# A recurrent scan step on Trainium2: one square moved to ScalarE, four activations reordered, and a common factor taken once

## The chip, the cores and the metric

The kernel runs on one core of a Trainium2 chip, as one program in one launch. The metric is the device time of a whole execution in microseconds (us). The engines are named as in the profile: PE is TensorE's matmul and PEld its weight load, DVE is VectorE, ACT is ScalarE, POOL is GpSimd and SP is SyncE. Each engine works through its own queue of instructions in order, and engines wait for each other (and for their own earlier results) on semaphores.

## What is computed

The reference is a small network of eight sublayers over x of 2 x 2048 x 256 numbers, in float32. The change touches only the first one, a gated scan over time. Its step, cut to what matters (h holds a complex number, as two real parts, for each of 2 batches, 256 channels d and 16 states n; there are 2048 steps):

```python
def step(h, inp):
    x_t, dt_t, B_t, C_t, xr_t = inp
    h_carrier = h.mean(axis=1)
    T = jnp.cos((c_phase(xr_t) - c_phase(h_carrier)) / 2.0) ** 2
    alpha = jnp.exp(dt_t[..., None] * A_neg)
    expo = 1.0 + (1.0 - alpha) * KAPPA * (1.0 - T[:, None, :])
    mag, ph = (c_mag(h), c_phase(h))
    cmag = jnp.minimum(jnp.exp(expo * jnp.log(mag + 1e-08)), 10.0)
    h = from_polar(cmag, ph)
    Bx = B_t[:, None, :, :] * (dt_t * x_t)[:, :, None, None]
    h = h + Bx
    h = from_polar(jnp.tanh(c_mag(h)), c_phase(h))
    y_t = jnp.einsum('bnc,bdnc->bd', C_t, h)
    return (h, y_t)
```

The lines of interest are the last three: a new h, here called p in the kernel, keeps its direction and gets the length tanh(|p|). The kernel computes this without angles. With m = |p| and e = exp(-2m), tanh(m) = (1 - e) / (1 + e), so the new h is p times (1/|p|) times (1 - e) times 1/(1 + e).

## The kernel before

The program goes through its sublayers one after the other: the tables for the scan, the scan, a projection, then routers, attention-like sublayers, a long convolution and feed-forward layers. Only the scan (`scan`, L257 to L549) and in it `step` (L400 to L488) is of interest here.

**Layout.** The 128 partitions hold batch, state and a quarter of the channels; the 64 columns (J) hold the channels of that quarter. Every tile of a step is 128 x 64, or 128 x 2 x 64 for the two parts of a complex number, and most instructions of a step work on 128 x 64 numbers.

**Order.** Steps depend on each other, so there are 2048 of them in sequence: a hardware loop (L513) of four passes, each with 32 groups (L517) of 16 unrolled steps (L539). The order of instructions on each engine is the order of the code, since the loop's body is under `manual_schedule`. Loads of the next group's tables are issued by SP at the start of a group. Two hooks fill gaps of a step with work for later steps: `act_gap` (called at L440) lets ACT compute the next step's input term bx (L391, twice) and in half of the steps a quarter of the next group's decay table (L385 or L387, 128 x 256); `dve_gap` (called at L454) lets DVE do small copies in a few steps.

**One step.** It begins with PE summing hs, the sums over channels of the last h (L410), and ACT and PE making from it the carrier's scale ci. Meanwhile DVE makes gl, ex and ngd (L414 to L425) from the logarithm lg and correction kd of the last step. ACT exponentiates (ea, fac). DVE forms p (L436 to L444), one instruction for each of the two parts. Then comes the stretch that the change touches:

- DVE: z and q[1], q[0] (squares of the parts, L446 to L449), m2 from z and q[1] (the squared magnitude with its small constant, L451), r1 from q[0] and q[1] (the same without it, L453).
- ACT: lm = ln m2 (L459), lr = ln r1 (L460), m = exp(lm / 2) (L461), ir = exp(-lr / 2), which is 1/|p| (L463), e = exp(-2m) (L464), lb (L466), le = ln(1 + e) (L468; its tile bears the name of m), sg = exp(-le), which is 1/(1 + e) (L469), then rm, k2c, ld and k1 (L470 to L473), which only the next step's lg and kd need.
- DVE: p times ir (L475, both parts), times (e - 1) (L477, both parts), and times sg (L480, both parts), the last with a sum over the columns into hs for the next step. Then th, kc, dl, lg and kd (L484 to L488), which make the logarithm and the correction for the next step.

The tiles lm, m, lr and lb lie in PSUM, the others in SBUF. The timeline of the profile calls the tile of both m and m2 "m", and those of r1 and k1 "r" and "k".

Of the kernel before, what the change touches and what calls it, by code (L numbers as in the profile page):

```python
# [17 lines left out]
AF = mybir.ActivationFunctionType  # L18
ALU = mybir.AluOpType
# [19 lines left out]
MAG_EPS = 1e-8  # L39
# [20 lines left out]
def new(pool, shape, name, **kw):  # L60
    return pool.tile(list(shape), F32, name=name, tag=name, **kw)


class Kernel:
# [192 lines left out]
    def scan(self, y, dtd, dxd, tabd):  # L257
# [7 lines left out]
        V, A, G = nc.vector, nc.scalar, nc.gpsimd  # L265
        J, TURN = 64, TG * GROUPS
        with ExitStack() as c:
# [129 lines left out]
            w = lambda sh, name: new(wp, [P, *sh], name)  # L397
            wa = lambda name: new(pa, [P, J], name)

            def step(k, g, before, act_gap, dve_gap):  # L400

                tc_, ng, dx, cs = tg[g]
                ng = ng[:, k]
                h = hist[g][:, k - 1] if k else hist[1 - g][:, TG - 1]
                hn = hist[g][:, k]
                i, o = (k + 1) % 2, k % 2

                for out in (hc, hd):
                    for r in range(0, P, 32):
                        nc.tensor.matmul(out[r : r + 32], mean[:, r : r + 32], hs[i], start=True, stop=True)  # L410
                before()

                gl, ex, ea, ngd = (w([J], n) for n in ("gl", "ex", "ea", "ngd"))
                V.tensor_tensor(gl, lg[i], ng, ALU.mult)  # L414


                sq, n2c = w([2], "sq"), w([1], "n2c")
                A.activation(sq, hc, AF.Square, accum_out=n2c)  # L418
                junk, dot = w([2], "junk"), w([1], "dot")
                V.tensor_tensor_reduce(  # L420
                    out=junk, in0=hd, in1=tc_[:, 4:6, k], scale=1.0, scalar=0.0, op0=ALU.mult, op1=ALU.add,
                    accum_out=dot,
                )
                V.tensor_tensor(ex, kd[i], gl, ALU.subtract)  # L424
                V.tensor_scalar(ngd, gl, dot, None, ALU.mult)  # L425
                ln, ci = wa("lr")[:, 0:1], w([1], "ci")
                A.activation(ln, n2c, AF.Ln, bias=1e-18)
                A.activation(ci, ln, AF.Exp, scale=-0.5)
                A.activation(ea, ex, AF.Exp)  # L429


                nc.tensor.matmul(hd[32:33, 0:1], ci, self.ident[:, 0:1], start=True, stop=True)  # L432


                p = w([2, J], "p")
                V.scalar_tensor_tensor(p[:, 0], h[:, 0], SMALL, ea, ALU.add, ALU.mult)  # L436
                V.tensor_tensor(p[:, 1], h[:, 1], ea, ALU.mult)  # L437
                fac = w([J], "fac")
                A.activation(fac, ngd, AF.Exp, scale=ci)  # L439
                act_gap(k)  # L440
                for k2 in range(2):
                    V.tensor_tensor(p[:, k2], p[:, k2], fac, ALU.mult)  # L442
                for k2 in range(2):
                    V.tensor_tensor(p[:, k2], p[:, k2], bx[o][:, k2], ALU.add)  # L444
                z = w([J], "z")
                V.scalar_tensor_tensor(z, p[:, 0], -2.0 * SMALL, p[:, 0], ALU.add, ALU.mult)  # L446
                q = w([2, J], "q")
                V.tensor_tensor(q[:, 1], p[:, 1], p[:, 1], ALU.mult)
                V.tensor_tensor(q[:, 0], p[:, 0], p[:, 0], ALU.mult)  # L449
                m2 = w([J], "m2")  # L450
                V.scalar_tensor_tensor(m2, z, MAG_EPS, q[:, 1], ALU.add, ALU.add)  # L451
                r1 = w([J], "r1")
                V.scalar_tensor_tensor(r1, q[:, 0], 1e-19, q[:, 1], ALU.max, ALU.add)  # L453
                dve_gap(k)  # L454

                lm, m, lr = wa("lm"), wa("m"), wa("lr")
                A.activation(lm, m2, AF.Ln)  # L459
                A.activation(lr, r1, AF.Ln)  # L460
                A.activation(m, lm, AF.Exp, scale=0.5)  # L461
                ir, e, sg, rm, ld = (w([J], n) for n in ("ir", "e", "sg", "rm", "ld"))
                A.activation(ir, lr, AF.Exp, scale=-0.5)  # L463
                A.activation(e, m, AF.Exp, scale=-2.0)  # L464
                lb, k1, k2c = wa("lb"), w([J], "k1"), w([J], "k2c")
                A.activation(lb, m2, AF.Ln, bias=MAG_EPS)  # L466
                le = wa("m")
                A.activation(le, e, AF.Ln, bias=1.0)  # L468
                A.activation(sg, le, AF.Exp, scale=-1.0)  # L469
                A.activation(rm, lm, AF.Exp, scale=-1.0)  # L470
                A.activation(k2c, lb, AF.Exp, scale=-0.5)
                A.activation(ld, e, AF.Ln, scale=-1.0, bias=1.0)  # L472
                A.activation(k1, rm, AF.Ln, scale=MAG_EPS, bias=1.0)  # L473
                for k2 in range(2):
                    V.tensor_tensor(p[:, k2], p[:, k2], ir, ALU.mult)  # L475
                for k2 in range(2):
                    V.scalar_tensor_tensor(p[:, k2], e, -1.0, p[:, k2], ALU.add, ALU.mult)  # L477
                th, kc, dl = (w([J], n) for n in ("th", "kc", "dl"))
                for k2 in range(2):
                    V.tensor_tensor_reduce(  # L480
                        out=hn[:, k2], in0=p[:, k2], in1=sg, scale=-1.0, scalar=0.0 if k2 else J * SMALL,
                        op0=ALU.mult, op1=ALU.add, accum_out=hs[o][:, k2 : k2 + 1],
                    )
                V.tensor_tensor(th, ld, le, ALU.subtract)  # L484
                V.scalar_tensor_tensor(kc, k2c, 2.0 * MAG_EPS, k1, ALU.mult, ALU.add)
                V.scalar_tensor_tensor(dl, hn[:, 0], -SMALL, rm, ALU.mult, ALU.mult)
                V.scalar_tensor_tensor(lg[o], th, 2.0, kc, ALU.mult, ALU.add)
                V.scalar_tensor_tensor(kd[o], kc, 0.5, dl, ALU.mult, ALU.add)  # L488
# [24 lines left out]
            with tc.For_i(0, S, TURN) as iv:  # L513
                A.preload_act_table_set(LOG_EXP)
                with tc.manual_schedule():
                    late = None
                    for g in range(GROUPS):  # L517
# [4 lines left out]
                        def act_gap(k):  # L522
                            for k2 in range(2):
                                if k + 1 < TG:
                                    drive(j, k + 1, k2, (k + 1) % 2)
                                else:
                                    drive(nxt, 0, k2, 0)
                            if k == 1:
                                rows(iv + (g + 1) * TG, nxt)
                            if 3 <= k < 11:  # L530
                                decay(nxt, (k - 3) // 2 * 4, 4, (k - 3) % 2)

                        def dve_gap(k):
                            if k == 1 and late is not None:
                                outputs(*late)
                            if k in (3, 4):
                                picked(nxt, k - 3)

                        for k in range(TG):  # L539
                            def before():  # L540
                                if k:
                                    project(j, k - 1, yps)
                                elif late is not None:
                                    project(1 - j, TG - 1, late[1])

                            step(k, j, before, act_gap, dve_gap)
# [1223 lines left out]
```

## Time and profile before

| what | value |
|---|---|
| time, median of 3 runs | 13,714.66 us (13,710.65 to 13,725.5) |
| the profiled execution's own time | 13,713.61 us |
| span of its trace | 13,711.9 us |
| DVE busy | 10,653.5 us, 78% of the span |
| ACT busy | 9,294.0 us, 68% |
| PE busy | 5,477.8 us, 40% |
| first and last start of L480 (the scan) | 370.5 and 10,034.5 us |

The shares are averages over the whole program. A row of a group gives the line, the engine, the operation, the tiles written and read, the shapes and the count; behind the first bar the busy time in all and the mean of one in ns; behind the second the idle time of the engine just before, and what ended it. A row of the timeline gives the start in us, the duration in us, engine, line, operation and tiles; in brackets the idle time before it. The span of an instruction on DVE or ACT overlaps that of the next one, so the distance from start to start, not the duration, is what an instruction occupies of its engine.

### The profile page before, as it was taken

What the parts mean: (1) busy time and instruction counts of PE and PEld (TensorE: products, weight loads), DVE (VectorE), ACT (ScalarE), POOL (GpSimd) and SP (SyncE); (2) the same over time, 40 slices, a digit from 0 to 9 for tenths busy, and PEclk for the clock granted to TensorE, in tenths of its full rate; (3) what the DMA queues carried; (4) which work ended last, traced back from release to release, by engine and by line L of the source; (5) the groups of instructions that cost most, each with busy time, mean ns of one, the idle gap of its engine ahead of it and who ended that gap; (6) DMA issues with size and microseconds to landing.
All of it is one profiled execution on the core that took longest, in us unless ns stands there. A gap on an engine that the chain in (4) does not pass through costs nothing. (4 is left out here: it accounts for less than half of the span.)

```text
span 13711.9 us, 263042 instructions
## 1 busy us (share of the span) xinstructions
PE 5477.8 (40%) x66344; PEld 3762.0 (27%) x66344; DVE 10653.5 (78%) x65491; ACT 9294.0 (68%) x45234; POOL 460.9 (3%) x528
## 2 busy tenths in 40 slices
PE   4222222222222222222222222222269867778888
PEld 2111111111111111111111111111135545644445
DVE  6888888888888888888888888888857677655555
ACT  3777777777777777777777777777735478534444
POOL 0000000000000000000000000000000001131110
PEclk6555555555555555555555555555559888889999
DMA  3000000000000000000000000000000045242210
GB/s 81 14 14 17 14 17 15 17 16 15 17 14 17 14 17 14 17 14 17 14 17 17 14 16 15 17 14 17 14 13 4 7 134 155 73 94 34 35 31 19
DMA packets 320440, 382.28 MB, mean 28 GB/s; under 512 B 207074, under 2 KB 230697, under 8 KB 317876
## 3 DMA queue, kind: packets, MB, share of 16 engines
q1 hardware_dynamic: 299444, 322.01, 10.2%
q0 software_dynamic: 17408, 42.75, 1.0%
q8 instruction: 533, 8.73, 0.3%
q14 instruction: 1007, 8.25, 0.2%
q10 hardware_dynamic: 2048, 0.53, 0.0%
HBM read 307.96 MB, written 52.46 MB: 26 GB/s over the span
## 5 line engine op out<-in xcount | busy, mean ns | idle before, releaser
L410 PE MATMUL hc<-hs,mean 128*32 128x2 f32 x16384 | 586.1, 203 | 7096.9 <-DVE hs L480 7033.2
L410 PEld LDWEIGHTS hc<-hs,mean 128*32 128x32 f32 x16384 | 410.6, 140 | 7308.9 <-DVE hs L480 7244.7
L475 DVE TENSOR_TENSOR p<-p,ir 128x64 f32<-128x64 f32 x4096 | 737.4, 221 | 1062.9 <-ACT ir L463 1062.9
L459 ACT ACTIVATE lm<-m 128x64 f32<-128x64 f32 x2048 | 466.2, 228 | 1210.2 <-DVE m L451 1210.2
L493 PE MATMUL yps<-cs,hist 128*64 128x8 f32 x8192 | 1224.9, 259 | 13.0 <-DVE hs L480 13.0
L391 ACT ACTIVATE bx<-dx,tc 128x64 f32<-128x64 f32 x4098 | 1169.4, 332 | 0.1
L1594 ACT ACTIVATE d_p<-ps_e 128x512 f32<-128x512 f32 (+3 forms) x1280 | 599.5, 537 | 754.2 <-PE ps_o L1575 534.8
L493 PEld LDWEIGHTS yps<-cs,hist 128*64 128x64 f32 x8192 | 1033.1, 218 | 45.1 <-DVE hs L480 13.4
L418 ACT ACTIVATE sq<-hc 128x2 f32<-128x2 f32 x2048 | 352.9, 172 | 795.2 <-PE hc L410 795.2
L480 DVE CUSTOM_DVE_ANT_0 hist<-p,sg 128x64 f32<-128x64 f32 x4096 | 761.0, 222 | 23.0 <-ACT rm L470 4.2
L477 DVE SCALAR_TENSOR_TENSOR p<-e,p 128x64 f32<-128x64 f32 x4096 | 738.1, 221 | 9.9 <-ACT sg L469 7.8
L442 DVE TENSOR_TENSOR p<-p,fac 128x64 f32<-128x64 f32 x4096 | 737.4, 221 | 8.9 <-DVE p L437 6.6
L444 DVE TENSOR_TENSOR p<-p,bx 128x64 f32<-128x64 f32 x4096 | 722.2, 218 | 2.6
L439 ACT ACTIVATE fac<-ngd,ci 128x64 f32<-128x64 f32 x2048 | 711.8, 348 | 1.0 <-DVE p L436 1.0
L436 DVE SCALAR_TENSOR_TENSOR p<-hist,ea 128x64 f32<-128x64 f32 x2048 | 459.7, 224 | 323.3 <-ACT ea L429 323.3
L429 ACT ACTIVATE ea<-ex 128x64 f32<-128x64 f32 x2048 | 524.3, 256 | 99.6 <-DVE ex L424 7.0
L1587 PE MATMUL ps_e<-d_qt,d_kt 128*128 128x512 f32 (+3 forms) x1280 | 556.4, 444 | 43.0 <-ACT d_p L1594 34.6
L472 ACT ACTIVATE ld<-e 128x64 f32<-128x64 f32 x2048 | 548.0, 268 | 0.0
L473 ACT ACTIVATE k<-rm 128x64 f32<-128x64 f32 x2048 | 545.0, 266 | 0.0
L410 PE MATMUL hd<-hs,mean 128*32 128x2 f32 x16384 | 543.7, 193 | 0.0
L1544 PE MATMUL ps_m<-d_kt,d_qt 128*128 128x512 f32 (+3 forms) x1280 | 499.3, 436 | 101.3 <-DVE d_part L1549 40.3
L432 PE MATMUL hd<-ident,ci 128*1 128x1 f32 x4096 | 386.7, 163 | 357.2 <-DVE ex L424 303.4
(453 smaller groups left out, 22720.5 us busy)
## 6 DMA issues: line engine op xcount, KB each, us to landing
toep<-in_C_krev SPq DMA_DIRECT2D x256, 312.0 KB, 5.5
ng<-dtd SPq DMA_DIRECT2D x258, 256.0 KB, 3.4
dx<-dxd SPq DMA_DIRECT2D x258, 256.0 KB, 3.9
d_kt<-d_kd SPq DMA_DIRECT2D x128, 128.0 KB, 4.1
d_qt<-d_qd SPq DMA_DIRECT2D x128, 128.0 KB, 3.7
y<-ys SPq DMA_DIRECT2D x512, 8.0 KB, 1.9
c_xd<-c_xs POOLq DMA_DIRECT2D x32, 256.0 KB, 2.6
c_yd<-c_ys POOLq DMA_DIRECT2D x32, 256.0 KB, 4.3
```

Source lines behind the costliest of these rows:

```text
L391: A.activation(bx[o][:, k2], tg[j][2][:, k], AF.Identity, scale=tg[j][0][:, k2, k : k + 1], bias=0.0 if k2 else SMALL,)
L410: nc.tensor.matmul(out[r : r + 32], mean[:, r : r + 32], hs[i], start=True, stop=True)
L439: A.activation(fac, ngd, AF.Exp, scale=ci)
L442: V.tensor_tensor(p[:, k2], p[:, k2], fac, ALU.mult)
L444: V.tensor_tensor(p[:, k2], p[:, k2], bx[o][:, k2], ALU.add)
L472: A.activation(ld, e, AF.Ln, scale=-1.0, bias=1.0)
L475: V.tensor_tensor(p[:, k2], p[:, k2], ir, ALU.mult)
L477: V.scalar_tensor_tensor(p[:, k2], e, -1.0, p[:, k2], ALU.add, ALU.mult)
L480: V.tensor_tensor_reduce(out=hn[:, k2], in0=p[:, k2], in1=sg, scale=-1.0, scalar=0.0 if k2 else J * SMALL, op0=ALU.mult, op1=ALU.add, accu ...
L493: nc.tensor.matmul(yps[:, k, :], hist[g][:, k, k2], tg[g][3][:, k2, k], start=k2 == 0, stop=k2 == 1)
L1587: nc.tensor.matmul(s[:, q0:], ks[kt // 4][:, hh, kt % 4 * P : (kt % 4 + 1) * P], q[:, hh, q0:], start=True, stop=not diag,)
L1594: A.activation(pr[:, q0:], s[:, q0:], AF.Exp, scale=0.25)
```

## The change

The square of the real part is computed by ACT, behind `act_gap`'s work, instead of DVE. On ACT, m comes ahead of lr, e ahead of ir, and le ahead of lb. The two multiplications by ir and the two by (e - 1) become one instruction that makes ai = (e - 1) times ir, and two multiplications by ai. A step so has two instructions fewer on DVE and one more on ACT. Nothing else of the program is changed, and the order on PE, POOL and SP stays as it was.

```diff
                 q = w([2, J], "q")
                 V.tensor_tensor(q[:, 1], p[:, 1], p[:, 1], ALU.mult)
-                V.tensor_tensor(q[:, 0], p[:, 0], p[:, 0], ALU.mult)
+                A.activation(q[:, 0], p[:, 0], AF.Square)
                 m2 = w([J], "m2")
...
                 A.activation(lm, m2, AF.Ln)
+                A.activation(m, lm, AF.Exp, scale=0.5)
                 A.activation(lr, r1, AF.Ln)
-                A.activation(m, lm, AF.Exp, scale=0.5)
                 ir, e, sg, rm, ld = (w([J], n) for n in ("ir", "e", "sg", "rm", "ld"))
+                A.activation(e, m, AF.Exp, scale=-2.0)
                 A.activation(ir, lr, AF.Exp, scale=-0.5)
-                A.activation(e, m, AF.Exp, scale=-2.0)
                 lb, k1, k2c = wa("lb"), w([J], "k1"), w([J], "k2c")
-                A.activation(lb, m2, AF.Ln, bias=MAG_EPS)
                 le = wa("m")
                 A.activation(le, e, AF.Ln, bias=1.0)
+                A.activation(lb, m2, AF.Ln, bias=MAG_EPS)
                 A.activation(sg, le, AF.Exp, scale=-1.0)
...
+                ai = w([J], "ai")
+                V.scalar_tensor_tensor(ai, e, -1.0, ir, ALU.add, ALU.mult)
                 for k2 in range(2):
-                    V.tensor_tensor(p[:, k2], p[:, k2], ir, ALU.mult)
-                for k2 in range(2):
-                    V.scalar_tensor_tensor(p[:, k2], e, -1.0, p[:, k2], ALU.add, ALU.mult)
+                    V.tensor_tensor(p[:, k2], p[:, k2], ai, ALU.mult)
                 th, kc, dl = (w([J], n) for n in ("th", "kc", "dl"))
```

## The prediction

> **What bounds the kernel now.** I read the page first: the span, and the costliest groups with what ended the idle time before them. Slices 2 to 30 of the page look alike, and the lines with x2048 and x4096 are the scan, so one step, 2048 times over, decides. The table of waits then shows a closed loop (PE waits for DVE's L480, ACT's L459 for DVE, DVE's L475 for ACT): a chain that hops between engines, where no engine is full. So I read one step in the timeline.
>
> ```profile
> span 13711.9 us, 263042 instructions
> ...
> L475 DVE TENSOR_TENSOR p<-p,ir 128x64 f32<-128x64 f32 x4096 | 737.4, 221 | 1062.9 <-ACT ir L463 1062.9
> ```
>
> ```profile
> 5004.20 0.22 DVE L414 TENSOR_TENSOR gl<-lg,ng 128x64 f32<-128x64 f32 x1
> ...
> 5004.45 0.23 DVE L424 TENSOR_TENSOR ex<-kd,gl 128x64 f32<-128x64 f32 x1
> ...
> 5005.67 0.49 ACT L385 ACTIVATE ng<-ng,aneg 128x256 f32<-128x256 f32 x1
> ...
> 5006.01 0.21 DVE L448 TENSOR_TENSOR q<-p 128x64 f32<-128x64 f32 x1
> 5006.15 0.21 DVE L449 TENSOR_TENSOR q<-p 128x64 f32<-128x64 f32 x1
> 5006.28 0.21 DVE L451 SCALAR_TENSOR_TENSOR m<-z,q 128x64 f32<-128x64 f32 x1
> 5006.42 0.21 DVE L453 SCALAR_TENSOR_TENSOR r<-q 128x64 f32<-128x64 f32 x1
> 5006.53 0.23 ACT L459 ACTIVATE lm<-m 128x64 f32<-128x64 f32 x1 [0.37 <-DVE m L451]
> 5006.69 0.21 ACT L460 ACTIVATE lr<-r 128x64 f32<-128x64 f32 x1
> 5006.84 0.18 ACT L461 ACTIVATE m<-lm 128x64 f32<-128x64 f32 x1
> 5006.94 0.21 ACT L463 ACTIVATE ir<-lr 128x64 f32<-128x64 f32 x1
> 5007.06 0.22 ACT L464 ACTIVATE e<-m 128x64 f32<-128x64 f32 x1
> 5007.17 0.23 ACT L466 ACTIVATE lb<-m 128x64 f32<-128x64 f32 x1
> 5007.19 0.36 DVE L475 TENSOR_TENSOR p<-p,ir 128x64 f32<-128x64 f32 x2 [0.56 <-ACT ir L463]
> 5007.31 0.22 ACT L468 ACTIVATE m<-e 128x64 f32<-128x64 f32 x1
> 5007.52 0.36 DVE L477 SCALAR_TENSOR_TENSOR p<-e,p 128x64 f32<-128x64 f32 x2
> 5007.57 0.22 ACT L469 ACTIVATE sg<-m 128x64 f32<-128x64 f32 x1
> 5007.69 0.22 ACT L470 ACTIVATE rm<-lm 128x64 f32<-128x64 f32 x1
> ...
> 5007.89 0.22 DVE L480 CUSTOM_DVE_ANT_0 hist<-p,sg 128x64 f32<-128x64 f32 x1
> ...
> 5008.04 0.27 ACT L473 ACTIVATE k<-rm 128x64 f32<-128x64 f32 x1
> ...
> 5008.34 0.22 DVE L485 SCALAR_TENSOR_TENSOR kc<-k2c,k 128x64 f32<-128x64 f32 x1
> ...
> 5008.89 0.22 DVE L414 TENSOR_TENSOR gl<-lg,ng 128x64 f32<-128x64 f32 x1
> ```
>
> The columns are start, duration, engine. gl to gl is 4.69 us; over the undisturbed steps it is 4.683 us, and 2048 steps make 9.59 ms of the 13,711.9 us span. Four prices are read here; the third decimals are those of the mean durations in the groups.
>
> 1. DVE, next instruction independent: start to start 0.135 us (6.01, 6.15, 6.28, 6.42), though each lasts 0.216.
> 2. DVE, next instruction needs the last one's result: ex needs gl and starts at gl's end plus 0.034 (4.20 + 0.218 + 0.034 = 4.45). An instruction takes 0.225 when it had to wait. So a dependent pair costs about 0.25 to 0.26 us, nearly twice the independent one. The kernel before almost never has such a pair in its step: q[0] stands between q[1] and m2, and each pair of parts (L475, L477) alternates.
> 3. A result of ACT is usable on DVE 0.033 us after its end (ir 6.94 + 0.215, L475 at 7.19), the same the other way (m2 to lm), and 0.032 on ACT itself (le 7.31 + 0.219, sg at 7.57). ACT issues the next instruction 0.103 us after an Exp (0.12 if the Exp had waited: sg to rm), and 0.146 after an Ln (lr to m, lb to le; 0.163 after a waiting one, lm to lr).
> 4. L480 waits for two engines. Its first half needs p[0] of L477, which ends at 7.52 + 0.225 = 7.745, and sg, which ends at 7.79. It starts 0.145 after p[0]'s end. L477, also a double wait, starts 0.106 after its p[0] of L475 ends (7.19 + 0.224). In each such case a semaphore instruction stands ahead of the waiting one (the query of L477's line lists 2048 of them).
>
> So the end of a step is set by the loop m2, lm, lr, ir, p times ir, p times (e-1), L480, then DVE's run th to gl.
>
> **The change, part by part** (same step, same clock).
>
> *Square of the real part to ACT.* ACT stands idle 0.37 us ahead of lm even in a step with the longest extra work, L385 (5.67 to 6.16). The real part is ready at about 5.61 + 0.218 + 0.033 = 5.86. The trace of before has no 64-wide Square. Nearest below is L418's at 0.172, above L439's Exp with a pointer scale at 0.348; I take 0.21. Even the longest, started at 6.16 behind L385, gives q[0] by 6.54; r1 would then end at 6.77 and lr could start at 6.80, and its slot (below) is 6.90. So the Square costs nothing; without ACT's idle time it would cost its issue slot, some 0.11. It can't gain of itself either. The Trainium skill (ScalarE: Activation LUTs, Rules for kernel authors) says that multiplication belongs on VectorE and not on ScalarE; by that the step would lose that slot of 0.11. The idle gap decides, so zero.
>
> *What DVE gets for it.* Not a slot of 0.135: m2 now stands directly behind q[1], which it needs. It starts at 6.01 + 0.216 + 0.034 = 6.26 instead of 6.28 and, having waited, lasts 0.225. lm starts at 6.26 + 0.225 + 0.033 = 6.518 against 6.53. Gain 0.01.
>
> *m ahead of lr.* m now waits for lm directly: 6.518 + 0.228 + 0.032 = 6.778 (before 6.84). lr follows a waiting Exp, 6.898 (before 6.69). e: the slot after an Ln, 6.898 + 0.146 = 7.044 (m has ended by 6.96; before 7.06). ir comes after e: 7.147 (lr ended at 7.107; before 6.94), ends 7.362. So e gains 0.02 and ir loses 0.21. le: e's end 7.262 + 0.032 = 7.294 (before 7.31). But lb now lies between le and sg: lb 7.457, sg 7.603 against 7.57. It ends at 7.826. rm, k2c, ld, k1 follow, the last at about 8.06, ending at 8.33.
>
> *(e - 1) / |p| once.* Four DVE instructions become three, but the first needs ir, the late one: ai at 7.362 + 0.033 = 7.395. Before, the two multiplications by ir ran at 7.19 while e and sg were being made; that overlap is gone. p[0] times ai needs ai: 7.395 + 0.224 + 0.034 = 7.653, ends at 7.877. L480: plus 0.145 = 8.02 instead of 7.89, that is 0.13 later. sg (7.83) is covered by this; if p[0] were in time, sg would allow 7.86 and be next.
>
> *Behind L480.* Before, th and kc waited for ACT's ld and k1 (8.04 + 0.266 + 0.033 = 8.34, kc's start). Now k1's result is there at 8.36 and kc would come at L480 + 0.297 + 0.135 = 8.45, so neither waits: 0.02 back. The queues of PE, POOL and SP and all DMA are untouched; PE's means follow L480 and shift with it.
>
> Sum: L480 0.13 later, 0.02 back, so 0.11 us a step; 2048 x 0.11 = 225 us. The profiled execution took 13,713.6 us (span 13,711.9), 1 us under the median of 13,714.7, so both give about **13,940 us**.
>
> A rule speaks against this sum. The Trainium skill (VectorE: DVE Perf Modes, The DRAIN you can't avoid, and Rules for kernel authors) holds that the next DVE instruction can't start before the pipe is empty anyway, a semaphore costing nothing extra, and advises to "Minimize op *count*, not sems". By it two instructions fewer save 2 x 0.135 x 2048 = 550 us: 13,160. The trace disagrees: independent neighbours start 0.135 apart while the first still runs to 0.216, and the dependent ex starts 0.252 after gl. I go by the rows.
>
> **Bounds of what is not shown.** L480's start after p[0]: 0.145 by its own row, 0.106 by L477's, which makes the step 0.07 longer: 13,857. I take L480's own, the same instruction. Upwards, the waits of m, e, ai and m2 are new, each costed by a like row. If these rows were 0.03 short in one of them, the step is 0.14 longer: 14,001. Below nothing isn't reached by these, as the two serial waits and the later ir each exceed the gain of 0.01.
>
> **Rivals.** *Dependent DVE neighbours cost only the slot.* Place: q[1] to m2, and ai to p[0]; price 0.135 to 0.144 instead of 0.25. Then m2 is at 6.15, lm 6.395, ir's end 7.24, ai 7.27, p[0] 7.416, L480 7.785: 0.105 sooner, with the 0.02 some 0.125 a step, 13,458, faster. It decides where the two pairs together cost under some 0.38 us. For it: the whole run z to r1 goes at 0.135; against it: ex behind gl, in every step. *sg sets the end*, and the products hide behind it: sg is 0.03 later, 0.02 comes back, 13,735, no change. For it: sg ends later than p[0] before; against it: L480 starts 0.10 after sg's end where other results of ACT are taken after 0.033. *ACT is dearer than costed*, by a Square that holds up lm or by longer slots around lr: over 14,005.
>
> **Chances.** The sum with its bounds 0.86, faster rival 0.05, no change 0.04, over 14,005 0.05. The range of 13,850 to 14,005 takes in the bounds and leaves out under 2 in 10. Faster or slower counts from 0.2% (27 us), about what a measurement of this kernel can tell from no change: faster 0.05, same 0.04, slower 0.91.
>
> **What would show it.** Right: gl to gl about 4.79; m2 0.25 behind q[1]; p[0] 0.26 behind ai; ai waiting for ir, not e, idle before it about 0.8 us; kc not waiting. Wrong: p[0] 0.14 behind ai, or L480 ended by sg, or lm waiting for the Square.

## The result and the profile after

The changed kernel takes 13,961.35 us, median of 4 runs (13,951.84 to 13,966.31), against 13,712.65 of the kernel before (median of 4 runs, one more than in the table of before): a ratio of 1.018, 95% interval 1.0165 to 1.0195. It is slower by about 249 us; the chain of the prediction had 225 (13,940 us, with a range of 13,850 to 14,005). The profiled execution of the changed kernel took 13,960.93 us, its trace spans 13,959.2.

First the page of the changed kernel: the span, the busy time and instructions of the engines, and the two groups of products with the idle time before them behind the last bar.

```profile
span 13959.2 us, 258946 instructions
...
PE 5469.9 (39%) x66344; PEld 3757.1 (27%) x66344; DVE 10301.9 (74%) x61395; ACT 9756.9 (70%) x47282; POOL 460.3 (3%) x528
...
L475 DVE SCALAR_TENSOR_TENSOR ai<-e,ir 128x64 f32<-128x64 f32 x2048 | 460.9, 225 | 1536.8 <-ACT ir L464 1536.8
...
L477 DVE TENSOR_TENSOR p<-p,ai 128x64 f32<-128x64 f32 x4096 | 738.4, 222 | 70.4
```

DVE has 4096 instructions and 352 us of work less than before, and the program is longer: DVE only waits more. Ahead of L475 it is idle 1536.8 / 2048 = 0.75 us a step, where it was 0.52, and the releaser is ir. The 70.4 us ahead of L477 are 0.034 us a step, with no other engine named: that is DVE waiting for its own ai.

Now one step in the timeline of the changed kernel (start, duration, engine, line). Its first gl, not shown, starts at 5004.10.

```profile
5005.76 0.26 ACT L449 ACTIVATE q<-p 128x64 f32<-128x64 f32 x1
...
5005.91 0.21 DVE L448 TENSOR_TENSOR q<-p 128x64 f32<-128x64 f32 x1
5006.16 0.23 DVE L451 SCALAR_TENSOR_TENSOR m<-z,q 128x64 f32<-128x64 f32 x1
...
5006.42 0.23 ACT L459 ACTIVATE lm<-m 128x64 f32<-128x64 f32 x1 [0.41 <-DVE m L451]
5006.68 0.21 ACT L460 ACTIVATE m<-lm 128x64 f32<-128x64 f32 x1
5006.80 0.22 ACT L461 ACTIVATE lr<-r 128x64 f32<-128x64 f32 x1
5006.95 0.22 ACT L463 ACTIVATE e<-m 128x64 f32<-128x64 f32 x1
5007.06 0.22 ACT L464 ACTIVATE ir<-lr 128x64 f32<-128x64 f32 x1
...
5007.31 0.23 DVE L475 SCALAR_TENSOR_TENSOR ai<-e,ir 128x64 f32<-128x64 f32 x1 [0.79 <-ACT ir L464]
...
5007.50 0.20 ACT L469 ACTIVATE sg<-m 128x64 f32<-128x64 f32 x1
5007.57 0.36 DVE L477 TENSOR_TENSOR p<-p,ai 128x64 f32<-128x64 f32 x2
...
5007.94 0.22 DVE L480 CUSTOM_DVE_ANT_0 hist<-p,sg 128x64 f32<-128x64 f32 x1
5007.96 0.26 ACT L473 ACTIVATE k<-rm 128x64 f32<-128x64 f32 x1
...
5008.37 0.22 DVE L485 SCALAR_TENSOR_TENSOR kc<-k2c,k 128x64 f32<-128x64 f32 x1
...
5008.91 0.22 DVE L414 TENSOR_TENSOR gl<-lg,ng 128x64 f32<-128x64 f32 x1
```

Three distances are to be seen. m2 stands 0.25 us behind q[1] where independent neighbours stand 0.135 apart. lr now begins 0.38 after lm (before 0.16), so ir is ready late, and ai starts 0.89 after lm, where the first product by ir started 0.66 after it. p[0] stands 0.26 behind ai. sg is done at 7.70, long before L480, so it is covered.

All steps are so alike that one number stands for a kernel: the median distance from gl to gl in its trace, called the step below. It is 4.683 us before and 4.810 after. The difference of 0.127 makes 260 us in 2048 steps; the two spans differ by 247.3. First gl to last gl grew by 256 us, since the steps off the median add up a little differently, and what lies around the scan took 9 us less.

### The profile page after: what moved, and what is told of

Read it like the earlier page. It is cut to its first block, busy times and chain, and to the rows that moved or that the text cites. A ratio compares the mean times of both kernels' runs of the same rounds, so it can differ in the third digit from the quotient of the medians.

```text
span 13959.2 us, 258946 instructions
## 1 busy us (share of the span) xinstructions
PE 5469.9 (39%) x66344; PEld 3757.1 (27%) x66344; DVE 10301.9 (74%) x61395; ACT 9756.9 (70%) x47282; POOL 460.3 (3%) x528
## 3 DMA queue, kind: packets, MB, share of 16 engines
q10 hardware_dynamic: 2048, 0.53, 0.0%
## 5 line engine op out<-in xcount | busy, mean ns | idle before, releaser
L475 DVE SCALAR_TENSOR_TENSOR ai<-e,ir 128x64 f32<-128x64 f32 x2048 | 460.9, 225 | 1536.8 <-ACT ir L464 1536.8
L477 DVE TENSOR_TENSOR p<-p,ai 128x64 f32<-128x64 f32 x4096 | 738.4, 222 | 70.4
L480 DVE CUSTOM_DVE_ANT_0 hist<-p,sg 128x64 f32<-128x64 f32 x4096 | 762.4, 223 | 25.0 <-ACT k L473 4.4
L449 ACT ACTIVATE q<-p 128x64 f32<-128x64 f32 x2048 | 508.1, 248 | 91.3 <-DVE p L444 6.7
```

What stands on the lines that cost most here:

```text
L477: V.tensor_tensor(p[:, k2], p[:, k2], ai, ALU.mult)
L480: V.tensor_tensor_reduce(out=hn[:, k2], in0=p[:, k2], in1=sg, scale=-1.0, scalar=0.0 if k2 else J * SMALL, op0=ALU.mult, op1=ALU.add, accu ...
```

## The experiments

The theory was the chain of the prediction: ir is made late, ai waits for it, p[0] waits for ai, and the end of the step follows. The rivals were that the Square takes ACT's time, that the number of DVE instructions counts or dependent neighbours cost nothing, and that sg sets the end. Each ratio is to runs of the kernel before on the same chip. The step is read from one trace of each kernel, and these traces are not all of one chip. The three parts alone and the run without the pair's wait, further down, share one; on it the stretch from gl to lm is some 0.006 us longer than in the other traces (2.337 to 2.338 against 2.330 to 2.332 with the Square on DVE, 2.325 to 2.326 against 2.319 to 2.321 with it on ACT). So the steps of these four compare among themselves as they stand, and with the others less about 0.006. First the parts alone and in pairs:

| kernel | ratio, 95% interval | step, us |
|---|---|---|
| before | 1 | 4.683 |
| Square alone | 0.9981 (0.9973 to 0.9989) | 4.679 |
| common factor alone | 1.0023 (1.0015 to 1.0031) | 4.712 |
| order alone | 1.0211 (1.0195 to 1.0226) | 4.838 |
| Square and factor | 1.0014 (1.0008 to 1.0021) | 4.694 |
| Square and order | 1.0196 (1.0179 to 1.0213) | 4.821 |
| order and factor | 1.0199 (1.0182 to 1.0216) | 4.821 |
| all three (the change) | 1.018 (1.0165 to 1.0195) | 4.810 |

**The Square alone.**

```diff
-                V.tensor_tensor(q[:, 0], p[:, 0], p[:, 0], ALU.mult)
+                A.activation(q[:, 0], p[:, 0], AF.Square)
```

> The kernel before with the Square alone (q[0] on ACT, all else as before). By the chain of rows: m2 stands behind q[1], which it needs, and starts 0.02 us sooner, lm 0.01 sooner; a step becomes 0.01 us shorter, 4.67 us, about 20 us in all: 13,693. Rival, the Square takes a slot of ACT from the chain: 0.11 us a step longer, about 13,940. Rival, a dependent neighbour on DVE costs only the slot of 0.135: 0.135 us a step shorter, about 13,440.

Measured 13,691.83 us, ratio 0.9981. The Square is hidden, and the slot that it frees on DVE is nearly all lost to the wait of m2 for q[1]. Both rivals fall. Against the trace of before the step shrank by 0.004 rather than 0.01, but that is the difference of the chips: beside the two other parts alone, from the same chip and with the Square on DVE, lm comes 0.012 and 0.011 sooner. That makes 23 to 25 us; the ratio makes 26 (its interval 15 to 37).

**The common factor alone.**

```diff
-                for k2 in range(2):
-                    V.tensor_tensor(p[:, k2], p[:, k2], ir, ALU.mult)
-                for k2 in range(2):
-                    V.scalar_tensor_tensor(p[:, k2], e, -1.0, p[:, k2], ALU.add, ALU.mult)
+                ai = w([J], "ai")
+                V.scalar_tensor_tensor(ai, e, -1.0, ir, ALU.add, ALU.mult)
+                for k2 in range(2):
+                    V.tensor_tensor(p[:, k2], p[:, k2], ai, ALU.mult)
```

> The kernel before with the common factor alone (ai, then two products; Square on DVE and the order of activations as before). By the chain: ai waits for e, which ends 0.11 us after ir in this order, so it starts 0.11 after the old L475; p[0] 0.26 behind it, L480 some 0.05 us later than before; th and kc no longer wait, 0.02 back: 0.02 to 0.03 us a step, about 13,760. Rival, a dependent neighbour costs only the slot: L480 is then ended by sg as before, no change, 13,713. Rival, the number of DVE instructions counts: one fewer, 0.135 a step, about 13,440.

Measured 13,747.81 us, ratio 1.0023; the step is 0.029 longer, or 0.023 without the chip's share, as the chain had it; the ratio makes 0.015. One DVE instruction fewer costs time, because ai must wait for the later of its two inputs, and p[0] for ai.

**The order alone.**

```diff
                 A.activation(lm, m2, AF.Ln)
+                A.activation(m, lm, AF.Exp, scale=0.5)
                 A.activation(lr, r1, AF.Ln)
-                A.activation(m, lm, AF.Exp, scale=0.5)
...
+                A.activation(e, m, AF.Exp, scale=-2.0)
                 A.activation(ir, lr, AF.Exp, scale=-0.5)
-                A.activation(e, m, AF.Exp, scale=-2.0)
```

(le goes ahead of lb as well, as in the change.)

> The kernel before with the new order of activations alone (m ahead of lr, e ahead of ir, le ahead of lb; four products as before, Square on DVE). By the chain: ir ends about 0.23 us later, the products by ir and by (e - 1) follow it unchanged, L480 0.23 later, 0.02 back behind it: 0.21 us a step, about 14,135. Rival, what sets the end is m, e and sg, which this order helps by 0.02: about 13,670.

Measured 14,009.02 us, ratio 1.0211: some 292 us longer and not 420. The direction is the chain's, the size is not. The timeline of this kernel tells why:

```profile
5000.90 0.36 DVE L475 TENSOR_TENSOR p<-p,ir 128x64 f32<-128x64 f32 x2 [0.79 <-ACT ir L464]
...
5001.18 0.35 DVE L477 SCALAR_TENSOR_TENSOR p<-e,p 128x64 f32<-128x64 f32 x2
```

L477 starts 0.28 us behind L475, where it was 0.33 before. e is now made ahead of ir on ACT, so the wait for ir covers it; L477 has only DVE left to wait for, and the semaphore instruction ahead of it is gone. The instructions of this line, first in the kernel before (the second row is the semaphore's), then with the new order:

```profile
L477 DVE SCALAR_TENSOR_TENSOR p<-e,p x4096: 215/224/226, 370.1 to 10034.1; 128x64 f32<-128x64 f32 x196
L477 DVEq EVENT_SEMAPHORE  x2048: 21/21/21, 370.1 to 10033.9; - x187
...
L477 DVE SCALAR_TENSOR_TENSOR p<-e,p x4096: 215/219/221, 368.2 to 10336.3; 128x64 f32<-128x64 f32 x196
```

Here the instruction that waits for two engines comes 0.05 us later than the same one that waits for one. I had read that price (0.106 from p[0]'s end to L477) and not seen that the order of activations removes it.

**Square and factor, with the old order.**

> The changed kernel with the old order of activations put back (Square and common factor stay). By the chain: ai waits for e instead of the late ir and starts about 0.11 us sooner than in the changed kernel, L480 with it; a step about 4.70 us, some 13,735, so that the order alone is worth 220 us of the loss. Rival, the common factor itself makes most of the loss: above 13,850.

Measured 13,726.73 us, ratio 1.0014, step 4.694. Putting the order back takes away 0.116 of the 0.127 us that the change costs. The rival falls.

**Order and factor, without the Square.**

> The changed kernel with the square of the real part back on DVE (new order and common factor stay). By the chain q[0] again fills the slot between q[1] and m2, lm is 0.01 us later, and nothing else moves: a step about 4.82 us, some 15 us more than the changed kernel: about 13,975. Rival, the Square on ACT was a part of the loss: less than 13,940.

Measured 13,977.02 us, ratio 1.0199, step 4.821. The Square helps by 0.011 us a step, here as forecast.

**Order and Square, with the four products.**

> The changed kernel with the four products put back (Square and new order stay). In the run of the order alone the first product by (e - 1) had one wait left instead of two, since e is made ahead of ir, which I had not costed; so from that run's step of 4.838 us, less 0.005 to 0.01 for the Square: 4.83 us, about 13,995, and the common factor is worth some 35 us in this order. Rival, the common factor's dependent pair makes most of the loss: below 13,900.

Measured 13,971.56 us, ratio 1.0196, step 4.821; the forecast of 4.83 started from the order alone, with its chip's share in it. In the new order the common factor gains 0.011, while in the old order it costs some 0.02 (0.015 to 0.029 in the table, where the chips are mixed). Where ir comes last, ai waits for nothing that the first product did not wait for too, and p[0] stands 0.26 behind ai, where L477 stands 0.28 behind the first product.

**The pair ai and p[0] without its wait.**

```diff
-                    V.tensor_tensor(p[:, k2], p[:, k2], ai, ALU.mult)
+                    V.tensor_tensor(p[:, k2], p[:, k2], e, ALU.mult)
```

> The changed kernel with the two products taken with e in place of ai (ai is still made, but nobody reads it, so the state is scaled by another factor than the reference's). Everything is issued in the same order; only the wait of p[0] for ai is gone. By the chain: p[0] starts 0.144 us behind ai instead of 0.259, L480 0.115 sooner, a step 4.695 us, some 236 us less than the changed kernel: about 13,725. Rival, the pair costs nothing beyond its slot: no change, 13,961.

Measured 13,743.73 us, ratio 1.002, step 4.706, 0.104 shorter than the change (0.11 without the chip's share; the ratios make 0.107) with the same instructions in the same places. Its timeline:

```profile
5003.01 0.23 DVE L475 SCALAR_TENSOR_TENSOR ai<-e,ir 128x64 f32<-128x64 f32 x1 [0.79 <-ACT ir L464]
...
5003.15 0.36 DVE L477 TENSOR_TENSOR p<-p,e 128x64 f32<-128x64 f32 x2
...
5003.65 0.26 ACT L473 ACTIVATE k<-rm 128x64 f32<-128x64 f32 x1
...
5003.95 0.23 DVE L485 SCALAR_TENSOR_TENSOR kc<-k2c,k 128x64 f32<-128x64 f32 x1
```

p[0] starts 0.14 behind ai instead of 0.26, so the dependence, not the slot, is what the pair costs. L480 comes 0.119 sooner by the medians, but the step shrinks by 0.104 only: k1 ends at 3.65 + 0.263, and kc starts 0.03 after that. ACT's tail is next in line.

**A version that uses what was found.** Two edits of the kernel before follow from the readings. The products are put in an order in which the third instruction has one wait left and no two dependent ones are neighbours:

```diff
-                for k2 in range(2):
-                    V.tensor_tensor(p[:, k2], p[:, k2], ir, ALU.mult)
-                for k2 in range(2):
-                    V.scalar_tensor_tensor(p[:, k2], e, -1.0, p[:, k2], ALU.add, ALU.mult)
+                V.tensor_tensor(p[:, 0], p[:, 0], ir, ALU.mult)
+                V.scalar_tensor_tensor(p[:, 1], e, -1.0, p[:, 1], ALU.add, ALU.mult)
+                V.scalar_tensor_tensor(p[:, 0], e, -1.0, p[:, 0], ALU.add, ALU.mult)
+                V.tensor_tensor(p[:, 1], p[:, 1], ir, ALU.mult)
```

> The kernel before with its four products in another order (p[0] times ir, p[1] times (e - 1), p[0] times (e - 1), p[1] times ir). The second instruction waits for e when e is just there, so that the third has one wait left, not two, and starts 0.28 us behind the first instead of 0.33: L480 0.05 sooner. By the chain that gains nothing yet, since kc, behind L480, still waits for ACT's k1, which is where it was: about 13,713. Rival, L480 alone sets the end: 0.05 us a step, about 13,610.

Measured 13,688.36 us, ratio 0.9987 (0.998 to 0.9993), step 4.688. L480 does come 0.058 us sooner, and nothing of it arrives:

```profile
5001.24 0.22 DVE L480 CUSTOM_DVE_ANT_0 hist<-p,sg 128x64 f32<-128x64 f32 x1
5001.30 0.27 ACT L472 ACTIVATE ld<-e 128x64 f32<-128x64 f32 x1
...
5001.45 0.27 ACT L473 ACTIVATE k<-rm 128x64 f32<-128x64 f32 x1
...
5001.60 0.22 DVE L484 TENSOR_TENSOR th<-ld,m 128x64 f32<-128x64 f32 x1
5001.75 0.23 DVE L485 SCALAR_TENSOR_TENSOR kc<-k2c,k 128x64 f32<-128x64 f32 x1
```

th starts 0.03 after ld's end and kc 0.03 after k1's. The gain on L480 became a wait for ACT. The small gain in time isn't the step's; it is taken up below.

The other edit fills the hole of 0.25 us between le and sg on ACT:

```diff
-                A.activation(sg, le, AF.Exp, scale=-1.0)
                 A.activation(rm, lm, AF.Exp, scale=-1.0)
+                A.activation(sg, le, AF.Exp, scale=-1.0)
```

> The kernel before with rm ahead of sg on ACT. le to sg is a wait of 0.25 us in which ACT issues nothing, so rm fits in for nothing, and k2c, ld and k1 come 0.10 us sooner. By the chain th and kc no longer wait for them: 0.02 us a step, about 13,665. Rival, rm delays sg and with it L480: 0.1 us a step longer, about 13,920.

Measured 13,659.14 us, ratio 0.9967 (0.9955 to 0.9979), step 4.659: 0.024 shorter, as expected. sg starts within 0.005 of where it did, and ld and k1 come 0.105 sooner.

Both together, without the Square:

> The kernel before with the products in the other order and rm ahead of sg, without the Square on ACT. If the two need each other (alone they gave little or 0.02 us a step), together they give some 0.085 of the 0.095 us by which the version with all three edits was shorter: a step about 4.60 us, some 13,525. Rival, the Square is what makes them work: above 13,600.

Measured 13,519.26 us, ratio 0.9864 (0.9848 to 0.9881), step 4.600. The two gave nothing and 0.024 alone and give 0.083 together.

With the Square as well:

> The kernel before with three edits: the Square on ACT, the four products in the other order, rm ahead of sg. By the chain L480 starts 0.05 us sooner, and th and kc are free of k1's wait, 0.02, and lm 0.01 sooner: 0.075 to 0.08 us a step, about 13,555. Rival, sg ends L480 as soon as the products are sooner: 0.03 us a step at most, about 13,650.

Measured 13,503.61 us, ratio 0.9853 (0.9838 to 0.9868), step 4.588, some 1.5% faster than the kernel before. The step is 0.095 us shorter and not 0.08: L480 comes 0.071 sooner (0.058 by the products, the rest by the Square), and 0.024 is gained behind it. Its timeline:

```profile
5005.01 0.22 DVE L474 TENSOR_TENSOR p<-p,ir 128x64 f32<-128x64 f32 x1 [0.56 <-ACT ir L463]
5005.13 0.22 ACT L468 ACTIVATE m<-e 128x64 f32<-128x64 f32 x1
5005.15 0.22 DVE L475 SCALAR_TENSOR_TENSOR p<-e,p 128x64 f32<-128x64 f32 x1
5005.29 0.21 ACT L469 ACTIVATE rm<-lm 128x64 f32<-128x64 f32 x1
5005.29 0.22 DVE L476 SCALAR_TENSOR_TENSOR p<-e,p 128x64 f32<-128x64 f32 x1
5005.39 0.22 ACT L470 ACTIVATE sg<-m 128x64 f32<-128x64 f32 x1
5005.42 0.22 DVE L477 TENSOR_TENSOR p<-p,ir 128x64 f32<-128x64 f32 x1
...
5005.65 0.22 DVE L480 CUSTOM_DVE_ANT_0 hist<-p,sg 128x64 f32<-128x64 f32 x1
...
5006.08 0.22 DVE L485 SCALAR_TENSOR_TENSOR kc<-k2c,k 128x64 f32<-128x64 f32 x1
```

All four products go at 0.135 to 0.14 apart, rm lies between le and sg, and kc follows L480 by 0.43 without a wait. It keeps the Square and drops the other two parts of the change.

## Why the prediction was right, step by step

*The Square costs nothing.* Right: lm waits for m2 and not for the Square, and ACT is idle 0.41 us ahead of lm in the step shown and at least 0.20 in every one of the 2048. It lasts 0.24 us and more (mean 0.248), longer than the 0.21 taken, within the bounds given. The run of the Square alone confirms it.

*What DVE gets for it is 0.01 us and not a slot of 0.135.* Right: lm comes 0.010 sooner against gl in the medians of the two traces. The rule of the Trainium skill that was weighed (VectorE: DVE Perf Modes, Rules for kernel authors: count operations, not semaphores) would, by the prediction's estimate, have made the change 550 us faster. The section from which the prediction took it (The DRAIN you can't avoid) says further that a next operation that is not held starts earlier, which the prediction left out; the 0.135 us between independent neighbours agrees with that. That a semaphore costs nothing extra was measured there on copies, and does not hold for the pair here. The run without the pair's wait settles it for this kernel: same number of instructions, 0.104 us a step less.

*ir later by 0.21.* Right: 0.211 in the start. Here lies what the sum lacked. lr and ir, each issued in its new place, last 0.223 us instead of 0.209 and 0.215, so ir is usable 0.015 later than forecast. L480 so came 0.150 later and not 0.13; 0.023 came back behind it, against 0.02 forecast. The step grew by 0.127 instead of 0.11. The term that was mis-sized is the duration of two activations, taken from their rows in the old order. The trace also tells which exchange made ir late: ir starts 0.031 behind the end of lr, which is the price of a result on ACT, so without e ahead of it it could have started no sooner. So it is the exchange of m and lr that makes ir late; that exchange was not run by itself.

*p[0] 0.26 behind ai, and 0.145 from its end to L480.* Right: 0.259 in the medians, and L480 starts 0.144 after p[0]'s end. The lower bound by L477's price of 0.106 was not needed. The price of a dependent pair had been read at ex, which is not gl's neighbour (L420 lies between them); the true neighbours, q[1] and m2 at 0.25 and ai and p[0] at 0.26, bear it out.

*What is next late.* Right in the change (kc waits for nothing there); the run without the pair showed how thin that cover is.

*What the sum couldn't tell.* The prediction laid the loss to the late ir and the serial pair together. The runs by parts divide it: with the other two in place the order costs 0.116, the Square gains 0.011 and the common factor gains 0.011. So the order makes the loss; the factor, which the prediction charged with the lost overlap, costs some 0.02, and only where ir comes ahead of e.

## What to carry to other kernels

In a chain that hops between engines, cost an edit by the start that it moves on the chain: each of the two instructions fewer on the busiest engine gained 0.011 us here and not a slot of 0.135, since the neighbours that remained depended on each other (0.25 to 0.26 us apart). Before two activations are swapped, ask which of their results the other engine takes first, and what it can do meanwhile. When a start is brought forward, look at once at the next wait behind it: two edits that give nothing and 0.5% of a step alone gave 1.8% together.

## What was not expected of the hardware

An instruction that waits for two engines started later than the same one that waits for one, though the other engine's result had long been there: by 0.05 us at L477, seen three times (it goes in the order alone, in Square and order, and in the new order of products). It goes without any wait being left out when an earlier instruction of the same engine has already waited for the later of two results of ACT.

An activation's duration depends on its neighbours: m lasts 0.177 us behind lr and 0.209 directly behind lm, lr 0.209 and 0.223. What sets it, no run here shows.

Some steps are longer than the median by more than 0.025 us. Without the starts and ends of the loop's four passes they are 236 in the trace of before, 55 us in all, and 156 with 34 us in the run of the other order of products. They are no accident: in each trace the same steps are late in all four passes (59 of 59 before, 39 of 39 there), so it is a matter of the place in the program. The spans of these two traces differ by 21.3 us, near the gain of 0.13%. Fewer late steps make 22 us of it, the median step takes 10 back, and the remaining 9 lie outside the scan, where the traces scatter between 4,029 and 4,047 us with the same code. In most late steps a DVE instruction is the first to start late, mostly by 0.15 to 0.36 us, and often with nothing that the profile shows to wait for. The profile of the version with three edits shows one, 0.18 us in brackets:

```profile
5010.39 0.22 DVE L480 CUSTOM_DVE_ANT_0 hist<-p,sg 128x64 f32<-128x64 f32 x1
5010.78 0.08 DVE L480 DVE_READ_ACCUMULATOR2_ANT hs<- 128x1 f32 x1 [0.18 <-issue]
```

What holds it was not tried and stays open.
